# Split-operand scores and head-laid keys for three of four token groups in the first 16-head attention of a fused transformer kernel

## The chip, the cores and the metric

The kernel runs on one core of one Trainium2 chip. The metric is the device time of one execution in microseconds (us); less is better. Before the change it is 921.34 us, the median of three runs (920.03 to 923.55).

A core has engines that run beside each other, each with a queue of its own: TensorE (PE in the profile; its weight loads are PEld), VectorE (DVE), ScalarE (ACT), GpSimd (POOL) and SyncE (SP), which here only issues DMAs. They share an on-chip memory of 128 partitions, and TensorE writes into a second, small one, PSUM, from which VectorE and ScalarE evict.

## The reference

Tokens `x` [32, 64, 128] (32 sequences of 64 tokens) and a context of the same shape go through four blocks, each an attention over the context and a feed-forward part, each added to `x` after a layernorm:

```python
x = x + L0_xattn(layernorm(x), ...);  x = x + L0_ffn(layernorm(x), ...)
x = x + L1_xattn(layernorm(x), ctx);  x = x + L1_ffn(layernorm(x), ...)   # mixture of experts
x = x + L2_xattn(layernorm(x), ctx, ctx);  x = x + L2_ffn(layernorm(x), ...)   # quantized
x = x + L3_xattn(layernorm(x), ctx, ctx);  x = x + L3_ffn(layernorm(x), ...)   # top 2 of 8 experts
```

The change is in `L2_xattn`, the first of two attentions with 16 heads of 8 channels: queries, keys and values are 128-channel projections with bias; in each sequence, each head takes softmax(q·k/√8 + mask) over the 64 keys (the mask is causal in this block), multiplies by the values, and the result is projected by `Wo`. All is float32.

## The kernel before

**Tiling.** The 2048 tokens are 4 groups (g = 0 to 3 in the code, groups 1 to 4 in the text) of 4 tiles of 128 tokens; a tile holds two sequences. `x` stays on chip throughout. `heads_xattn` runs a 16-head block: for each group `heads_inputs` (L1205) makes queries, for each tile `heads_tile` (L1230) does the attention. `i` is 0 for this block and 1 for the second one of the kind, which uses the same code.

**Context.** `heads_context` (L1148) makes, for a group, the values `hv` (a split product at L236 by `mm3`, masked on VectorE at L1173) and by `heads_keys` (L1127) the keys `hk`: one product for each half of the channels (L1134), evicted by ScalarE with the bias (L1144). The keys stand in [channel, token] layout, 64 channels (8 heads) for each of two halves, and twice along the partitions, once for each sequence of a tile. `hv`'s constant columns are set on GpSimd (L1156, L1157).

**Queries.** `queries` (L1196) normalises a group on VectorE (L183), turns it on TensorE (L204) and copies it on ScalarE (L1201, `hqnT`). `heads_inputs` multiplies it by `Wq` (L1222) and evicts four pieces of 64x256 into `hq`: for each half one on VectorE (L1226) and one on ScalarE (L1227), in places such that each sequence's queries meet only that sequence's rows. The rest of `hq` is zero, set once by two memsets (L1124).

**Tile.** GpSimd builds `kb` (L1244): the tile's keys times a mask of heads, 128x1024, so that each of the 8 heads of a half has its own 64 columns with only its 8 channels not zero. Then for each half TensorE adds the mask (L1257, bfloat16) and the score (L1258): queries as the weights, `kb` as the moving operand, 512 columns, in plain float32, which the profile shows as two matmul records. VectorE takes the maximum (L1259) and subtracts it (L1260), ScalarE takes the exponential of both halves (L1261), TensorE transposes 8 blocks (L1268), ScalarE copies them (L1269), TensorE multiplies by the values (L1275), VectorE divides by the sums (L1283, L1284). At a group's end the result is turned (L204), copied (L1298, `hoT`), projected by `Wo` (L1305) and added (L1299, L1306).

**Split products.** Elsewhere the kernel writes a float32 number as a high part, rounded to the type float32r, and a low remainder, and takes three products, `mm3` (L233): high·high, low·high, high·low, each one matmul (the rows L236 and L917).

**Order.** Parts of the work are generators. `interleave` (L98) keeps three tiles in flight here and puts steps of later work (`K.behind`: next group's inputs, weights of the next stage) between them. Over that, the tile framework plans the order on each engine from a modelled timeline; `in_turn` pins the order of a few instructions. The stage before (the mixture of experts, with lines such as L917 to L1016) and this one overlap at their border. Loads go out on SP; the last layer's expert weight `W_raw` is loaded and split (L1490 to L1492) within this stage.

Of the kernel before, what the change touches and what calls it, by code (L numbers as in the profile page):

```python
# [18 lines left out]
F32 = mybir.dt.float32  # L19
# [1100 lines left out]
def heads_room(K, pool):  # L1120

    K.hq = [pool.tile([P, 2, GT, 2, S], F32, name=f"hq{i}") for i in range(2)]
    for t in K.hq:
        K.nc.gpsimd.memset(t, 0.0)  # L1124


def heads_keys(K, pool, i, g, tags):  # L1127

    nc = K.nc
    kT = pool.tile([P, 2, GT, S], F32, name=f"hk{i}{g}")  # L1130
    for half in range(2):
        ps = bank(K, tags[half], [P, GT, 2, S])
        w = K.wkp[i][:, half, :, :].rearrange("p r f -> p (r f)")
        step = nc.tensor.matmul(ps.rearrange("p t b s -> p (t b s)"), w, K.ctxT[g], start=True, stop=True)  # L1134
        if i:
            in_turn(K, [K.l2_last, step])
            K.l2_last = step
        for b in range(2):
            rows = slice(b * S, (b + 1) * S)
            bias = col(K, f"{HEAD_BLOCKS[i]}_bk2", half)[rows, :]  # L1140
            if i and b in KEY_DVE:
                nc.vector.tensor_scalar(kT[rows, half, :, :], ps[rows, :, b, :], bias, None, ALU.add)
            else:
                nc.scalar.activation(kT[rows, half, :, :], ps[rows, :, b, :], AF.Identity, bias=bias)  # L1144
    K.hk[i][g] = kT


def heads_context(K, pool, tp, g, tags):  # L1148
# [4 lines left out]
    hv = K.hv[g] = pool.tile([P, 2 * GT, 2, 8, 2, 9], F32, name=f"hv{g}")  # L1153
# [4 lines left out]
    heads_keys(K, pool, 0, g, tags)  # L1158
# [22 lines left out]
def heads_pools(K, stack, i, side):  # L1181
    b = HEAD_BLOCKS[i]
    return SimpleNamespace(**{
        n: stack.enter_context(K.tc.tile_pool(name=f"{b}_{n}", bufs=bufs, side=at, reuse_waits="tile"))
        for n, bufs, at in (("op", 2, "left"), ("gp", 2, "left"), ("ep", EP[i], side), ("pp", PP[i], side))
    }, kp=K.kp)
# [9 lines left out]
def queries(K, pool, i, g, tags=("hqn", "hqnT")):  # L1196

    qn = normed(K, pool, K.x[g], "hqn", tag=tags[0], stats=None if i else K.l2ln[g], after=K.queried if g and not i else None)
    ps = turned(K, qn, QN[i])
    qnT = pool.tile([P, GT, 2, S], F32, name="hqnT", tag=tags[1])  # L1200
    K.nc.scalar.copy(qnT, ps.rearrange("p (t b s) -> p t b s", b=2, s=S))  # L1201
    return qnT


def heads_inputs(K, C, g):  # L1205
# [10 lines left out]
    yield  # L1216
    ps = bank(K, QN[C.i], [P, 2, GT, S])
# [6 lines left out]
    for half in range(2):  # L1224
        bias = K.hbq[:, C.i, half : half + 1]
        K.queried = nc.vector.tensor_scalar(hq[0:S, half, :, 0, :], ps[0:S, half, :, :], scale, bias[0:S, :], ALU.mult, ALU.add)  # L1226
        nc.scalar.activation(hq[S:P, half, :, 1, :], ps[S:P, half, :, :], AF.Identity, bias=bias[S:P, :], scale=scale)  # L1227


def heads_tile(K, C, g, t):  # L1230
# [8 lines left out]
    if t == AHEAD[C.i] and g + 1 < NG:  # L1239
        K.behind.insert(0, C.inputs[g + 1])  # L1240
    hq, o = K.hq[g % 2], C.o
    kb = C.kp.tile([P, 2, 8, S], F32, name="kb")
    full = [P, 2, 8, S]
    step = nc.gpsimd.tensor_tensor(  # L1244
        kb, K.hk[C.i][g][:, :, t, :].unsqueeze(2).to_broadcast(full),
        K.head.unsqueeze(1).unsqueeze(3).to_broadcast(full), ALU.mult,
    )
    if C.i:
        in_turn(K, [K.l2bo_step, step])
    K.kb_step = step  # L1250
# [3 lines left out]
    for half in range(2):  # L1254
        ps = bank(K, SCORES[C.i][half], [P, 8, S])
        heads = slice(half * 8, half * 8 + 8)
        nc.tensor.matmul(ps, K.identb, K.masks[C.i], start=True, stop=False)  # L1257
        nc.tensor.matmul(ps, hq[:, half, t, :, :].rearrange("p b s -> p (b s)"), kb[:, half, :, :], start=False, stop=True)  # L1258
        nc.vector.tensor_reduce(nm[:, heads], ps, AX.X, ALU.max, negate=True)  # L1259
        nc.vector.tensor_tensor(e[:, heads, :], ps, nm[:, heads].unsqueeze(2).to_broadcast([P, 8, S]), ALU.add)  # L1260
# [36 lines left out]
    oT = C.op.tile([P, GN], F32, name="hoT")[:, : n * P]  # L1297
    nc.scalar.copy(oT, ps)  # L1298
    step = nc.gpsimd.tensor_tensor(xg, xg, K.hbo[C.i].unsqueeze(1).to_broadcast([P, n, P]), ALU.add)  # L1299
    if C.i == 0 and g < NG - 1:  # L1300
# [184 lines left out]
def l3_ffn_weights(K, pool, tmp):  # L1485
    parts = []
    for name, n, src in (("gate", 8, "L3_ffn_gate_w"), ("W3", 1024, "L3_ffn_weight")):
        hi, lo = (pool.tile([P, n], F32R, name=f"{name}_{part}") for part in ("hi", "lo"))
        raw = tmp.tile([P, n], F32, name=f"{name}_raw")
        K.nc.sync.dma_start(raw, K.ins[src])  # L1490
        in_turn(K, [K.normed, K.nc.vector.tensor_copy(hi, raw)])
        K.nc.gpsimd.tensor_tensor(lo, raw, hi.bitcast(F32), ALU.subtract)  # L1492
# [64 lines left out]
def fused_kernel(ctx: ExitStack, tc: tile.TileContext, ins: dict, out: bass.AP):  # L1557
# [17 lines left out]
    K.hk = [[None] * NG, [None] * NG]  # L1575
    K.moe_stack = ExitStack()
# [9 lines left out]
    with ExitStack() as inner:  # L1586
        late, late_k, K.late_v, x_pool = (
            inner.enter_context(tc.tile_pool(name=n, bufs=1, reuse_waits="tile")) for n in ("late", "late_k", "late_v", "l2_x")
        )
        heads_room(K, late)  # L1590
# [5 lines left out]
        K.kp = ctx.enter_context(tc.tile_pool(name="kp", bufs=KB_BUFS, side="right", reuse_waits="tile"))  # L1596
        wp = ctx.enter_context(tc.tile_pool(name="l3f_w", bufs=1, side="right", reuse_waits="tile"))
        with ExitStack() as stack:
            l2_pools = heads_pools(K, stack, 0, "right")
# [4 lines left out]
            K.behind.clear()  # L1604
        l2_stack = ExitStack()
        K.l2p = l2_stack.enter_context(tc.tile_pool(name="l2f_w", bufs=1, side="right", reuse_waits="tile"))
        head_pools = heads_pools(K, inner, 1, "left")
        with tc.tile_pool(name="l2f", bufs=2, reuse_waits="tile") as gp:
            keys = lambda g: heads_keys(K, late_k, 1, g, KEY_TAGS)
# [101 lines left out]
```

## Time and profile before

| | |
|---|---|
| median of 3 runs | 921.34 us (920.03 to 923.55) |
| profiled execution | 922.2 us |
| its span in the profile | 920.5 us |
| mean granted TensorE clock | 0.967 |
| PE / PEld / DVE / ACT / POOL busy | 826.2 / 675.7 / 744.5 / 559.5 / 328.7 us |
| the stage's score products, L1258 | first at 630.2, last at 717.4 us |
| two records of a score product | 0.86 us from the first's start to the next instruction's |
| `kb` on GpSimd, L1244 | x32 (16 in this stage), mean 1.98 us |
| exponential, L1261 | x32, mean 1.06 us |

All are rows of one profiled execution; the span is the time between its first and last instruction, and 1.7 us of the execution lie outside. A row such as "L1258 PE MATMUL s_ps<-kb,hq 128*128 128x512 f32 x2" gives line, engine, operation, output and inputs, shape and count. "<-ACT hq" after a row's idle time names the instruction whose end released it. Matmul records overlap, so what a matmul costs in a full row of them is the distance from start to start.

### The profile page before, as it was taken

The numbers are of one execution on the slowest core, as the hardware profiler recorded it, in microseconds if no ns is written. First come the engines' busy times: TensorE is split into PE (matmuls) and PEld (weight loads), VectorE is DVE, ScalarE is ACT, GpSimd is POOL, SyncE is SP. The second block draws the span as 40 slices with busy tenths as digits, with TensorE's granted clock in tenths as the row PEclk, the third lists the DMA queues.
The fourth block names the chain that finished last, engine by engine and source line by source line (L and its number), as shares of the span: only waits on it lengthen the run. The fifth ranks groups of instructions, "written<-read, shape, count | busy, mean of one in ns | idle before, by whom it ended". The sixth has DMA issues, their size and how long they took to land.

```text
span 920.5 us, 15730 instructions
## 1 busy us (share of the span) xinstructions
PE 826.2 (90%) x5833; PEld 675.7 (73%) x5838; DVE 744.5 (81%) x1888; ACT 559.5 (61%) x1082; POOL 328.7 (36%) x300
## 2 busy tenths in 40 slices
PE   3978999998999998899999799997999789898995
PEld 3878999997998876687787688674676447566673
DVE  5989899698779767877678877789788878779877
ACT  3545676666667579596678767564545483445432
POOL 3744465253323323511040311014465303436342
PEclk9999999999999999999999999998999999899978
DMA  7320000000000000001000000000000000000000
GB/s 188 92 85 21 1 13 13 12 1 1 1 13 1 1 14 0 15 1 33 1 1 1 1 1 1 0 24 1 1 1 1 2 0 1 2 1 1 13 13 23
DMA packets 22669, 13.73 MB, mean 15 GB/s; under 512 B 3008, under 2 KB 21952, under 8 KB 22592
## 3 DMA queue, kind: packets, MB, share of 16 engines
q1 hardware_dynamic: 18320, 10.62, 4.2%
q10 hardware_dynamic: 4272, 2.10, 0.9%
q8 instruction: 46, 0.75, 0.3%
q14 instruction: 31, 0.25, 0.1%
HBM read 11.66 MB, written 1.05 MB: 14 GB/s over the span
## 4 chain that ended last, share of the span: by engine, by line
PE 49%; DVE 27%; ACT 15%; issue 3%; POOL 2%; DMA 2%; SPq 0%; ACTq 0%; DVEq 0%; POOLq 0%
PE c_ps L917 6%; PE g_ps L479 5%; PE s_ps L1258 4%; PE s_ps L445 4%; PE c_ps L236 4%; PE g_ps L236 3%; PE c_ps L1268 2%; PE g_ps L1275 2%; PE t_ps L465 2%; PE s_ps L236 2%; ACT L940 2%; PE t_ps L236 2%; ACT L935 1%; DVE mh_lo L894 1%; DVE nm L447 1%
## 5 line engine op out<-in xcount | busy, mean ns | idle before, releaser
L461 POOL TENSOR_TENSOR e<-e,rs 128x512 f32<-128x512 f32 x64 | 66.0, 1041 | 98.9 <-DVE rs L460 53.4
L161 POOL TENSOR_TENSOR ln_rstd<-ln_rs,neghalf 128x4 f32<-128x4 f32 (+1 forms) x38 | 40.5, 1067 | 144.0 <-DVE ln_rs L169 135.8
L1244 POOL TENSOR_TENSOR kb<-hk,head 128x1024 f32<-128x1024 f32 x32 | 63.2, 1978 | 72.7 <-PE s_ps L1258 57.3
L1258 PE MATMUL s_ps<-kb,hq 128*128 128x512 f32 x128 | 68.9, 623 | 5.4 <-ACT hq L1227 5.2
L445 PE MATMUL s_ps<-kvT,G 128*128 128x128 f32 x512 | 71.6, 277 | 1.8 <-DVE e L451 1.8
L445 PEld LDWEIGHTS s_ps<-kvT,G 128*128 128x128 f32 x512 | 65.6, 192 | 6.0 <-issue 1.8
L917 PE MATMUL c_ps<-mh_hi,w2e_hi 128*128 128x512 f32 x160 | 61.7, 425 | 4.6 <-ACT be L935 2.7
L479 PE MATMUL g_ps<-N,Ct 128*128 128x128 f32 x512 | 61.7, 275 | 0.0
L479 PEld LDWEIGHTS g_ps<-N,Ct 128*128 128x128 f32 x512 | 60.1, 192 | 0.7
L1259 DVE TENSOR_REDUCE nm<-s_ps 128x8 f32<-128x512 f32 x64 | 43.6, 681 | 18.9 <-PE s_ps L1258 18.5
L1269 ACT COPY hpT<-c_ps 128x512 f32<-128x512 f32 x64 | 35.4, 591 | 33.7 <-PE c_ps L1268 33.6
L473 ACT COPY Ct<-c_ps 128x512 f32<-128x512 f32 x64 | 38.2, 598 | 28.6 <-PE c_ps L236 22.7
L469 DVE TENSOR_TENSOR pT_lo<-t_ps,pT_hi 128x512 fp32r<-128x512 f32 x64 | 43.3, 680 | 14.8 <-ACT pT_hi L468 12.5
L1261 ACT ACTIVATE e<-e 128x1024 f32<-128x1024 f32 x32 | 34.0, 1063 | 34.4 <-DVE e L1260 32.0
L1275 PEld LDWEIGHTS g_ps<-hv,hpT 128*64 128x64 f32 x1024 | 36.1, 144 | 22.9 <-issue 8.4
L917 PE MATMUL c_ps<-mh_hi,w2e_lo 128*128 128x512 f32 x160 | 52.1, 403 | 0.0
L894 DVE TENSOR_TENSOR mh_lo<-m,mh_hi 128x1024 fp32r<-128x1024 f32 x32 | 40.4, 1261 | 14.3 <-ACT mh_hi L893 13.4
L452 ACT ACTIVATE e<-e 128x512 f32<-128x512 f32 x56 | 35.4, 640 | 24.5 <-DVE e L451 24.0
L917 PE MATMUL c_ps<-mh_lo,w2e_hi 128*128 128x512 f32 x160 | 49.4, 404 | 0.5 <-DVE mh_lo L894 0.5
L425 ACT COPY G<-g_ps 128x512 f32<-128x512 f32 x60 | 35.9, 598 | 21.4 <-PE g_ps L236 20.4
L468 ACT CAST pT_hi<-t_ps 128x512 fp32r<-128x512 f32 x64 | 37.8, 594 | 17.2 <-PE t_ps L465 10.7
L962 POOL TENSOR_TENSOR be<-be 128x256 f32<-128x256 f32 x16 | 16.9, 1055 | 80.9 <-DVE tg L967 80.3
(519 smaller groups left out, 2689.0 us busy)
## 6 DMA issues: line engine op xcount, KB each, us to landing
kv_tok<-in_x ACTq DMA_DIRECT2D x8, 128.0 KB, 3.3
kv_tok<-in_ctx SPq DMA_DIRECT2D x8, 128.0 KB, 2.9
x<-in_x SPq DMA_DIRECT2D x4, 256.0 KB, 8.2
ctx<-in_ctx SPq DMA_DIRECT2D x4, 256.0 KB, 3.2
w2e_raw<-in_L_ffn_expert_w SPq DMA_DIRECT2D x1, 768.0 KB, 4.4
out<-x SPq DMA_DIRECT2D x3, 256.0 KB, 2.3
WkT<-in_L_xattn_WkT ACTq DMA_DIRECT2D x2, 256.0 KB, 6.4
WqT<-in_L_xattn_WqT SPq DMA_DIRECT2D x2, 256.0 KB, 6.2
```

Source lines behind the costliest of these rows:

```text
L161: K.nc.gpsimd.tensor_tensor(out, v, K.neghalf.to_broadcast(list(v.shape)), ALU.pow)
L236: step = K.nc.tensor.matmul(ps, w[a], x[b], start=start and i == 0, stop=stop and i == 2)
L445: nc.tensor.matmul(ps[:, j, :], G[:, bb, h : h + 2, :].rearrange("p h s -> p (h s)"), kvT[:, bb, :], start=True, stop=True)
L461: nc.gpsimd.tensor_tensor(e, e, rs.unsqueeze(2).to_broadcast([P, 4, P]), ALU.mult)
L469: nc.vector.tensor_tensor(lo, ps, hi.bitcast(F32), ALU.subtract)
L479: nc.tensor.matmul(ps, Ct[:, h, :], C.N[:, h, :], start=(h == 0), stop=(h == 15))
L894: nc.vector.tensor_tensor(lo, m, hi.bitcast(F32), ALU.subtract)
L917: nc.tensor.matmul(ps, K.w2p[part][:, 2 * n + i, cols], x[:, i, :, :], start=first, stop=last)
L1244: step = nc.gpsimd.tensor_tensor(kb, K.hk[C.i][g][:, :, t, :].unsqueeze(2).to_broadcast(full), K.head.unsqueeze(1).unsqueeze(3).to_broadca ...
L1258: nc.tensor.matmul(ps, hq[:, half, t, :, :].rearrange("p b s -> p (b s)"), kb[:, half, :, :], start=False, stop=True)
L1259: nc.vector.tensor_reduce(nm[:, heads], ps, AX.X, ALU.max, negate=True)
L1275: nc.tensor.matmul(po[b * S : (b + 1) * S, j, :, :].rearrange("p r d -> p (r d)"), pT[:, j, b * S : (b + 1) * S], K.hv[g][:, 2 * t + b, C. ...
```

## The change

It touches this block only, and in it the scores of groups 2 to 4; group 1 keeps `kb` and the float32 product.

- **Scores.** For groups 2 to 4 the score is three split products through `mm3` in place of one float32 product.
- **Queries.** In this block all four pieces are evicted on ScalarE. For groups 2 to 4 they go into a plain tile `hqf`; ScalarE copies each to a high part and GpSimd subtracts the low part, into a tile `hqp` with both parts (one for two groups each, zeroed by a memset of 128x2048; groups 2 and 4 share one).
- **Keys.** The keys of groups 2 to 4 are split once for a group (`key_parts`: high copy on ScalarE, low on GpSimd, 128x512 each). Two tiles `kbd` of 128x4096, zeroed once by GpSimd, hold the keys laid out by head for two token tiles each. They are filled by 16 DMAs on SP (8 heads × 2 sequences; 8 partitions × 512 numbers each) for each pair of tiles, in all 6 pairs and 96 DMAs. The twelve `kb` of these groups fall away.
- **Room and order.** Group 1's `kb` shares its place with the last group's values; `hqnT` and `hoT` have one buffer in place of two; the second block's keys take the places of the split keys, and its query tiles are zeroed when its groups begin; the last layer's expert weight is loaded and split in two halves of 512 columns; some `in_turn` pins are dropped, and normalising of group 2 no longer waits for the queries of group 1.

The diff, cut to its core:

```diff
+def key_rooms(K, pool):
+    K.kbd = []
+    for n in range(2):
+        K.kbd.append(zero(K, pool.tile([P, 8, 2, 2, 2, S], F32R, name=f"kbd{n}")))
+        if n == 0:
+            key_parts(K, 1)
+        yield
+
+def key_parts(K, g):
+    kT = K.hk[0][g]
+    parts = K.hks[g] = K.late_k.tile([P, GT, 2, 2, S], F32R, name=f"hks{g}", tag=f"hks{g}")
+    K.nc.scalar.copy(parts[:, :, 0, :, :], kT)
+    K.nc.gpsimd.tensor_tensor(parts[:, :, 1, :, :], kT, parts[:, :, 0, :, :].bitcast(F32), ALU.subtract)
+
+def lay_keys(K, g, pair):
+    kb = K.kbd[pair % 2]
+    for h in range(8):
+        for b in range(2):
+            rows = slice(b * S + 8 * h, b * S + 8 * h + 8)
+            K.nc.sync.dma_start(kb[rows, h, :, :, :, :].bitcast(F32), K.hks[g][rows, 2 * pair : 2 * pair + 2, :, :, :].bitcast(F32))
+    return kb
...
 def heads_inputs(K, C, g):
...
+        if C.i == 0:
+            for b in range(2):
+                rows = slice(b * S, (b + 1) * S)
+                out = hqf[rows, half, :, :] if parts else hq[rows, half, :, b, :]
+                K.queried = nc.scalar.activation(out, ps[rows, half, :, :], AF.Identity, bias=bias[rows, :], scale=scale)
+                if parts:
+                    hi, lo = (hqp[rows, part, half, :, b, :] for part in range(2))
+                    nc.scalar.copy(hi, out)
+                    nc.gpsimd.tensor_tensor(lo, out, hi.bitcast(F32), ALU.subtract)
+            continue
...
 def heads_tile(K, C, g, t):
...
+    parts = C.i == 0 and g > 0
+    if parts:
+        if t % 2 == 0:
+            K.kb = lay_keys(K, g, t // 2)
+        kb = K.kb
+    else:
...
+        if parts:
+            queries = tuple(hq[:, part, half, t, :, :].rearrange("p b s -> p (b s)") for part in range(2))
+            mm3(K, ps, queries, tuple(kb[:, :, t % 2, part, half, :] for part in range(2)), False, True)
+        else:
+            nc.tensor.matmul(ps, hq[:, half, t, :, :].rearrange("p b s -> p (b s)"), kb[:, half, :, :], start=False, stop=True)
...
-    if C.i == 0 and g < NG - 1:
+    if (C.i, g) == (0, 0):
         in_turn(K, [K.kb_step, step])
...
-        raw = tmp.tile([P, n], F32, name=f"{name}_raw")
-        K.nc.sync.dma_start(raw, K.ins[src])
-        in_turn(K, [K.normed, K.nc.vector.tensor_copy(hi, raw)])
-        K.nc.gpsimd.tensor_tensor(lo, raw, hi.bitcast(F32), ALU.subtract)
+        for cols in [slice(at, min(at + 512, n)) for at in range(0, n, 512)]:
+            raw = tmp.tile([P, cols.stop - cols.start], F32, name=f"{name}_raw")
+            K.nc.sync.dma_start(raw, K.ins[src][:, cols])
+            in_turn(K, [K.normed, K.nc.vector.tensor_copy(hi[:, cols], raw)])
+            K.nc.gpsimd.tensor_tensor(lo[:, cols], raw, hi[:, cols].bitcast(F32), ALU.subtract)
```

## The prediction

> **What bounds it now.** I read the busy times first, then the chain of work that ended last, then the stage alone.
>
> ```profile
> PE 826.2 (90%) x5833; PEld 675.7 (73%) x5838; DVE 744.5 (81%) x1888; ACT 559.5 (61%) x1082; POOL 328.7 (36%) x300
> ...
> PE 49%; DVE 27%; ACT 15%; issue 3%; POOL 2%; DMA 2%; SPq 0%; ACTq 0%; DVEq 0%; POOLq 0%
> ```
>
> TensorE is busy nine tenths of the span, but only half of the chain that sets the end is its own; VectorE and ScalarE hold most of the rest. So work taken off TensorE pays only where neither of these is late. The table by stretches shows the stage (first score product at 630, last at 718, in us from the span's start):
>
> ```profile
> 622.00:640.00 18.00, 11.84 (x49) 6.42 (x49) 15.85 (x32) 7.89 (x14) 9.72 (x12) 0.81 0.01 1
> 640.00:660.00 20.00, 19.82 (x183) 13.90 (x182) 17.04 (x39) 11.18 (x18) 9.92 (x7) 1.00 0.00 1
> 660.00:680.00 20.00, 20.00 (x208) 14.45 (x208) 15.63 (x39) 10.71 (x19) 9.16 (x6) 1.00 0.01 2
> 680.00:700.00 20.00, 19.12 (x192) 13.28 (x192) 18.59 (x47) 8.01 (x13) 13.83 (x11) 1.00 0.00 1
> 700.00:722.00 22.00, 21.07 (x222) 14.07 (x221) 17.84 (x45) 11.45 (x18) 7.76 (x6) 1.00 0.01 1
> ```
>
> Columns: length, then busy us of PE, PEld, DVE, ACT, POOL, the granted clock, DMA. From 640 TensorE is full (19.1 to 20.0 of 20), VectorE next (15.6 to 18.6). Only the start is different, and TensorE's waits from 615 to 731 name it:
>
> ```profile
> PE s_ps L1258 <- ACT hq L1227: 5.2, 1, 5.2
> PE s_ps L1257 <- DVE e L1260: 1.3, 3, 0.8
> PE n_ps L1222 <- ACT hqnT L1201: 0.9, 1, 0.9
> ```
>
> One wait of 5.2 us for the first queries; after it waits add up to some 3 us in 100.
>
> **The products.** The timeline shows how matmuls of 512 columns follow each other, in float32 split operands (L917) and in the plain float32 score (L1258):
>
> ```profile
> 614.72 0.62 PE L917 MATMUL c_ps<-mh_hi,w2e_lo 128*128 128x512 f32 x2
> 615.18 0.63 PE L917 MATMUL c_ps<-mh_hi,w2e_hi 128*128 128x512 f32 x2
> 615.65 0.62 PE L917 MATMUL c_ps<-mh_hi,w2e_lo 128*128 128x512 f32 x2
> ...
> 641.20 1.02 PE L1258 MATMUL s_ps<-kb,hq 128*128 128x512 f32 x2
> 642.06 0.60 PE L204 MATMUL n_ps<-ident,W_inT 128*128 128x128 f32 x4
> ```
>
> Start to start, two split products take 0.465 us, one 0.2325, three 0.70; one float32 score (two records) takes 642.06 − 641.20 = 0.86. The gain is 0.16 for a product, and groups 2 to 4 have 3 × 4 tiles × 2 halves = 24: **−3.8 us** of TensorE. The other bound is the records' own lengths: 3 × about 0.41 (L917, mean 403 to 425 ns) = 1.23 against 2 × 0.59 (L1258's shorter records) = 1.18, so +0.05 × 24 = +1.2. Pipelined matmuls overlap, so I take the pacing. The split keys are read in runs of 64 columns; the trace has no split product of that layout.
>
> **The start.** Queries are evicted one half on VectorE (L1226), one on ScalarE (L1227), and ScalarE's stood behind VectorE's: ScalarE was idle 15.3 us over eight L1227 rows, released by L1226. Now all four follow the product on ScalarE, 0.47 each (L1227), idle there from 623.9 to 629.6. The first score can start at about 627 instead of 630.2. But in the built program's order the second score tile now follows the tail of the MoE stage and the next queries, which VectorE still paces (15.85 of 18), and VectorE gets 1.7 us of next-group work earlier (normalising, 4 tiles at 1.06, and the low context part, 0.68). Following the rows through, group 2 begins 0.8 to 1.4 us earlier: **−1.1**. Ends: 0 (VectorE takes all) and −6.1 (5.2 + 0.9, all kept).
>
> **VectorE and GpSimd.** VectorE loses eight evictions of about 0.42. GpSimd loses twelve key blocks of 1.98 (L1244), −23.8; it gains two zeroed key tiles of 4096 columns at four times the 0.94 of a 1024-column memset (7.5), two query tiles of 2048 (3.7), twelve low query parts of at most 0.77 (a subtraction of 128x256; 9.2) and three low key parts of 1.3 (3.9): +24.3. So it is as busy as before, but earlier. Beside a key block VectorE's normalising slows, 2.13 us for four tiles at 696.35 against 1.02 to 1.10 alone; that goes: **−1.1**. Ends: 0, and −3 if each of the three groups gains so.
>
> **ScalarE.** It gains 8 evictions × 0.47, 12 high query parts × 0.47, 3 high key parts × 0.6: 11.2 us on 54.8 of 111. It has room, but the work comes in bursts where a group changes: four evictions, four casts, four key evictions and a key part stand ahead of an exp (L1261, 1.06) which the transposes need. I follow one late exp in group 2: **+1.5** on TensorE. From group 2 on a group's first score waits for an eviction, a cast (0.47) and a subtraction (up to 0.77) in a row, 1.24 more than for an eviction. At the change from group 3 to 4, where an exp and other evictions stand in front, TensorE's waits of before (0.34 at 701.31 and 0.25 at 702.20) become about 2.5 by my count of the rows: **+1.9**. Ends for both together: 0 (score tiles in flight cover them) and +6 (as much at each group).
>
> **The keys' DMAs.** Each pair of tiles needs 16 transfers within the on-chip memory, of 8 rows × 2 KB = 16 KB, all issued from SP; six pairs, 96. No row of before shows such a transfer. SP's small loads stand at 34.44, 34.91 and 35.39, and at 374.76 and 375.22: 0.46 to 0.48 apart; ends 0.37 (414.43 to 414.80) and 0.68 (373.60 to 374.28). Landing of small loads takes 1.6 to 2.5. So a pair takes 16 × 0.48 + 2 = 9.7 us (ends 7.5 and 13.4). In the built program each transfer waits for the landing of the eighth before it, so a landing of over 8 × 0.48 = 3.8 would stretch the row too. What is queued on SP behind these waits: only the next pairs, and the second half of the last layer's expert weight, which is loaded between groups 3 and 4 and waits for GpSimd to have read the first half (684 in before, L1492), so group 4's first pair cannot go before that. A pair can start when the pair before the last has been read, and a tile takes TensorE about 5 us. Following it through: zeroing ends near 637.4, the low key part of group 2 near 644.7, its first pair lands near 654 and is needed near 658; the later ones land 3 to 6 us ahead. I cost them at **0**; the cover is that slack. Behind a score that waits stand, on TensorE, the next tiles' masks, transposes and value products, and through them VectorE. TensorE has to wait on the several semaphores of a pair: about 4 waits × 51 ns (event rows on PE's sequencer) × 6 = 1.2 at most, I take **+0.6**.
>
> A rule speaks against this. The Trainium skill, "DMA: Bandwidth & Descriptors", section "Measured (HBM→SBUF, 128 partitions, SWDGE, issued from GpSimd)", says that transfers under 64 KB are dominated by descriptors and should be batched; its section "Anatomy of one DMA — SWDGE (gpsimd) path" gives a fixed 2.0 us for each. If these added up one after another, a pair would take 16 × 2.04 = 33 us, an estimate from that page, and the sum would end about 100 us later. The loads issued 0.48 apart above overlap their landings, which speaks for 9.7; whether transfers within the on-chip memory do so, no run here shows.
>
> **Sum.** −3.8 − 1.1 − 1.1 + 1.5 + 1.9 + 0.6 = −2.0. From the second feed-forward on (731) the program's order is the same, so the difference is kept. The profiled execution took 922.2 (span 920.5 and 1.7 around it); it becomes 920.2. The median of the three runs is 0.9 below the profiled one: **919.3**.
>
> **Rivals.** About 0.5% (4.6 us) is what a measurement here can tell from no change.
> - *Larger gain* (chance 0.22): the start's 6.1 us stay won, the products' 3.8 too, and the bursts are covered: −5 to −12. For it: the 5.2 us are the stage's only large idle. Against: VectorE at 15.85 of 18 there, which still has the MoE tail to end.
> - *Slower, the DMA issue on SP* (0.18): if an issue with its share of landing takes over 0.70 us, a pair takes over 13 us and eats its slack; from there each 0.1 us costs 16 × 0.1 = 1.6 for a pair, 9.6 for six. At 0.8 to 0.95: +8 to +22, so 929 to 943. For it: the loads at 373.60 (0.68), untried transfers, one queue. Against: the 0.48 of most.
> - *The query chain becomes the wait* (0.13): ScalarE and GpSimd are late at each group, the +6 in place of 3.4, and the start's gain goes: 0 to +5, 921 to 926.
> - *It does not do what it says* (0.07): three split products on strided keys cost what the float32 one costs (+1.2 in place of −3.8): 922 to 925.
> - *Forecast* (0.40): −1 to −5, 916.3 to 920.3.
>
> Faster by over 0.5%: 0.08 of the forecast and 0.22, together 0.30. Slower: 0.18, 0.04 of the query chain, 0.01 of the last, together 0.23. The rest 0.47. The range takes the larger gain down to −11 and the DMA case up to +11, leaving out about 0.16: 910 to 932. The forecast's own range is 916 to 920.5.
>
> **What would show it.** TensorE's start to start over three L1258-kind products: 0.70, or more. The wait for queries of 5.2 gone. SP's issues 0.45 to 0.5 apart, landings 2 us; a TensorE wait released by a DMA before a score of groups 2 to 4 would prove the slower rival, and its length gives its price. An exp waiting behind query casts shows the bursts. GpSimd near 56 us in the stage, VectorE some 5 below. A difference beyond 731 would prove me wrong about the rest. I am wrong in kind if the DMA packets slow other engines, which no row here could tell.

## The result, and the profile after

After the change the kernel takes 927.55 us (median of 6 runs, 926.0 to 929.51), before 921.63 on the same chips (6 runs, 920.03 to 923.55): ratio 1.0063, interval 1.0046 to 1.0080. It is 0.6% slower, by 5.9 us. The forecast was 919.3, so the direction was wrong; the time lies in the range.

The profiled execution took 926.0 (span 924.3), the fastest of the six, so its trace explains 3.8 us, not all 5.9. The stage, from the end of the mixture of experts to the second feed-forward's first transposes, went from 114.6 to 120.4 us (+5.8), what follows from 184.1 to 182.6, what precedes from 621.8 to 621.3. From the page after, busy times and the chain's shares by engine:

```profile
PE 827.5 (90%) x5859; PEld 681.6 (74%) x5862; DVE 747.9 (81%) x1881; ACT 569.1 (62%) x1105; POOL 326.8 (35%) x309
...
PE 51%; DVE 25%; ACT 16%; issue 3%; DMA 2%; POOL 2%; SPq 1%; ACTq 0%; DVEq 0%; POOLq 0%
```

Totals hardly move. The stage's table after, with the stretches and columns of before (length, busy PE, PEld, DVE, ACT, POOL, granted clock, DMA share, GB/s):

```profile
622.00:640.00 18.00, 11.45 (x44) 6.06 (x44) 15.89 (x27) 8.30 (x19) 12.57 (x10) 0.81 0.01 1
640.00:660.00 20.00, 18.78 (x144) 12.63 (x145) 16.69 (x35) 13.00 (x20) 14.33 (x16) 1.00 0.08 16
660.00:680.00 20.00, 19.72 (x220) 15.69 (x218) 16.11 (x42) 11.18 (x21) 5.01 (x6) 1.00 0.13 25
680.00:700.00 20.00, 19.00 (x215) 15.57 (x216) 17.38 (x40) 11.41 (x18) 6.16 (x7) 1.00 0.17 38
700.00:722.00 22.00, 20.76 (x209) 15.75 (x209) 15.14 (x41) 11.82 (x21) 8.05 (x9) 0.84 0.09 17
```

Two rows differ in kind. From 640 to 660 TensorE does 1.04 us less and 144 matmul records instead of 183: the stage starts late. From 700 the granted clock is 0.84 where it was 1.00. TensorE's longest waits after, from 615 to 731 (us in total, times, longest):

```profile
PE n_ps L204 <- DVE x L1017: 2.0, 1, 2.0
PE n_ps L249 <- DVE w_in L137: 1.9, 1, 1.9
PE c_ps L1347 <- ACT e L1340: 1.3, 2, 1.0
PE s_ps L1337 <- ACT hq L1283: 1.2, 1, 1.2
```

The wait of 5.2 for the first queries is 1.2 now (the forecast had it gone), but the first score starts at 629.9 instead of 630.2: others took its place. VectorE's timeline after shows the largest:

```profile
631.99 0.69 DVE L1338 TENSOR_REDUCE nm<-s_ps 128x8 f32<-128x512 f32 x1 [1.17 <-PE s_ps L1337]
632.59 0.41 DVE L984 SCALAR_TENSOR_TENSOR xnext<-step,xnext 128x256 f32<-128x256 f32 x1
633.41 0.69 DVE L1338 TENSOR_REDUCE nm<-s_ps 128x8 f32<-128x512 f32 x1 [0.40 <-PE s_ps L1337]
634.02 4.19 DVE L183 TENSOR_SCALAR hqn<-x,ln_mv,ln_rstd 128x128 f32<-128x128 f32 x4
638.67 1.44 DVE L1002 TENSOR_SCALAR halt<-halt 128x256 f32<-128x256 f32 x1 [0.46 <-ACT halt L1001]
...
642.50 1.28 DVE L1339 TENSOR_TENSOR e<-s_ps,nm 128x512 f32<-128x512 f32 x2
```

The maxima of the two halves of group 1's first tile are ready at 632.7 and 634.1, but their subtractions (L1339) come only at 642.5. Before, maximum and subtraction are neighbours:

```profile
632.65 0.67 DVE L1259 TENSOR_REDUCE nm<-s_ps 128x8 f32<-128x512 f32 x1
633.25 0.40 DVE L984 SCALAR_TENSOR_TENSOR xnext<-step,xnext 128x256 f32<-128x256 f32 x1
633.59 0.67 DVE L1260 TENSOR_TENSOR e<-s_ps,nm 128x512 f32<-128x512 f32 x1
```

Tile 2's score moves from 635.7 to 643.9, group 2's first from 653.3 to 662.7, in these rows of before and after:

```profile
653.33 1.02 PE L1258 MATMUL s_ps<-kb,hq 128*128 128x512 f32 x2
662.68 1.64 PE L236 MATMUL s_ps<-kbd,hqp 128*128 128x512 f32 x6
```

So from the stage's start to group 2's first score it takes 41.4 us where it took 31.5, and from there to the stage's end 79.0 where it took 83.1: the whole loss lies ahead of group 2.

Between the maximum and the subtraction stands the normalising, 4.19 us where four tiles take 1.02 to 1.10 alone, and the end of the mixture of experts (L1002 to L1017). The normalising lies beside this GpSimd row after:

```profile
630.96 7.11 POOL L1128 MEMSET kbd<- 128x4096 f32 x2 [5.39 <-DVE step L983]
```

The longest of the four normalising instructions takes 3.61 us, as long as one memset (3.59); the shortest 0.35. "SBUF — State Buffer" of the Trainium skill, section "SBUF: two separate sides", calls the ports that VectorE and GpSimd share an exclusive lock: where a VectorE instruction needs them, the one that starts first holds them for the whole instruction, with the other blocked. These rows agree. Which of the two holds the subtraction, VectorE's work or something else, they don't tell.

**The clock.** In these stretches of the timeline of after (same columns) the clock is the column before the last two:

```profile
622.70:626.10 3.40, 1.05 (x4) 0.44 (x4) 3.40 (x7) 0.03 (x1) 2.83 (x5) 1.00 0.00 0
626.10:629.50 3.40, 1.98 (x8) 0.79 (x8) 3.40 (x11) 1.24 (x3) 0.00 (x0) 0.51 0.00 0
...
704.60:708.10 3.50, 2.41 (x25) 1.54 (x24) 0.17 (x1) 3.26 (x7) 2.59 (x5) 0.99 0.12 23
708.10:714.90 6.80, 6.80 (x33) 4.66 (x32) 4.63 (x9) 1.64 (x2) 0.60 (x1) 0.50 0.11 22
...
738.80:742.20 3.40, 0.55 (x5) 0.56 (x6) 3.37 (x8) 1.49 (x2) 1.65 (x1) 1.00 0.00 0
742.20:745.60 3.40, 3.18 (x11) 1.65 (x11) 2.39 (x6) 1.45 (x3) 0.00 (x0) 0.50 0.00 0
```

The clock halves in whole steps of 3.41 us, each time after a step that TensorE's records filled only in part (0.16 to 0.68 of it in the three places shown). The stage holds 7.2 us of half clock before (626.8 to 633.6 and a little of 736.0 to 739.4) and 17.1 after: 626.1 and 708.1 for 6.8 each, 731.9 for 3.4. If TensorE does half its work then, the additional 9.9 us cost 5.0 of the 5.8, an estimate. The remaining 0.8 would be what it lost in waits less what it saved in products.

### The profile page after: what moved, and what is told of

It reads as the page before. It is cut to its first block, busy times and chain, and to the rows that moved or that the text cites. A ratio compares the mean times of both kernels' runs of the same rounds, so it can differ in the third digit from the quotient of the medians.

```text
span 924.3 us, 15939 instructions
## 1 busy us (share of the span) xinstructions
PE 827.5 (90%) x5859; PEld 681.6 (74%) x5862; DVE 747.9 (81%) x1881; ACT 569.1 (62%) x1105; POOL 326.8 (35%) x309
## 4 chain that ended last, share of the span: by engine, by line
PE 51%; DVE 25%; ACT 16%; issue 3%; DMA 2%; POOL 2%; SPq 1%; ACTq 0%; DVEq 0%; POOLq 0%
PE c_ps L917 5%; PE g_ps L479 5%; PE s_ps L445 4%; PE c_ps L236 4%; PE g_ps L236 4%; PE s_ps L236 3%; PE s_ps L1337 3%; PE g_ps L1354 3%; PE t_ps L236 2%; PE t_ps L465 2%; PE c_ps L1347 2%; ACT L940 2%; DVE mh_lo L894 2%; DVE m L892 1%; ACT L935 1%
## 5 line engine op out<-in xcount | busy, mean ns | idle before, releaser
L1348 ACT COPY hpT<-c_ps 128x512 f32<-128x512 f32 x64 | 34.8, 591 | 31.4 <-PE c_ps L1347 31.2
L1340 ACT ACTIVATE e<-e 128x1024 f32<-128x1024 f32 x32 | 34.0, 1064 | 30.9 <-DVE e L1339 28.5
L1319 POOL TENSOR_TENSOR kb<-hk,head 128x1024 f32<-128x1024 f32 x20 | 38.1, 1907 | 36.1 <-PE s_ps L1337 33.2
L468 ACT CAST pT_hi<-t_ps 128x512 fp32r<-128x512 f32 x64 | 37.7, 594 | 16.7 <-PE t_ps L465 10.2
L236 PE MATMUL g_ps<-latT_hi,A_hi 128*128 128x256 f32 x120 | 38.9, 324 | 7.6 <-DVE latT_hi L213 4.8
L893 ACT CAST mh_hi<-m 128x1024 fp32r<-128x1024 f32 x32 | 33.4, 1045 | 19.8 <-DVE m L892 18.2
```

Source lines behind the costliest of these rows:

```text
L236: step = K.nc.tensor.matmul(ps, w[a], x[b], start=start and i == 0, stop=stop and i == 2)
L1319: step = nc.gpsimd.tensor_tensor(kb, K.hk[C.i][g][:, t, :, :].unsqueeze(2).to_broadcast(full), K.head.unsqueeze(1).unsqueeze(3).to_broadca ...
```

## The experiments

**Theories.** *Order and rooms* (mine after reading the trace; a tile's room is the address that it gets): the two zeroed key tiles push the exponentials' tile `e` from address 156096 to 131520 (bytes in a partition of the on-chip memory, in the built program), where the end of the mixture of experts still has its tiles. Tile 1's `e` ends at 135616, and `halt`, written at L1002 and read at L1007, starts at 135392. So tile 1's subtraction must wait for L1007. *VectorE held*: GpSimd's zeroing does it. *ScalarE's load*, *DMA issue*: the forecast's rivals. *Half clock* (later): the emptied steps are a cause of their own. *Key supply* (later): 96 transfers in a row are a second bound.

All times are medians with the interval of the ratio to the kernel before, run on the same chip (921.0 to 922.1). "Stage" and "half" are, from the profiled execution, the stage's length and the half-clock time in it. The edits are shortened to their core.

| kernel | us | ratio | stage | half |
|---|---|---|---|---|
| before | 921.63 | | 114.6 | 7.2 |
| after | 927.55 | 1.0046 to 1.0080 | 120.4 | 17.1 |
| e1_zero_pieces | 930.47 | 1.0058 to 1.0105 | 127.2 | 27.3 |
| e2_old_evict | 937.59 | 1.0141 to 1.0183 | 132.5 | 34.1 |
| e3_lay_once | 927.97 | 1.0038 to 1.0076 | 120.3 | 14.9 |
| e4_ahead1 | 931.39 | 1.0078 to 1.0119 | 124.0 | 27.3 |
| e5_pin_norm | 934.24 | 1.0079 to 1.0167 | 125.6 | 23.9 |
| e6_pin_kbd_late | 932.21 | 1.0089 to 1.0148 | 126.0 | 20.5 |
| e7_scalar_evict_only | 922.88 | 0.9994 to 1.0031 | 116.2 | 10.1 |
| e8_f32_laid | 930.67 | 1.0073 to 1.0116 | 124.4 | 14.6 |
| e9_zero_scalar | 932.35 | 1.0112 to 1.0158 | 130.5 | 27.3 |
| e10_zero_dma | 929.16 | 1.0076 to 1.0126 | 123.7 | 17.1 |
| e11_rooms_only | 931.04 | 1.0075 to 1.0126 | 122.3 | 20.1 |
| e12_exp_rooms | 928.25 | 1.0037 to 1.0078 | 123.2 | 20.5 |
| e13_before_pad | 929.22 | 1.0041 to 1.0094 | 124.2 | 15.2 |
| e14_high_only_f32 | 926.87 | 1.0029 to 1.0074 | 120.7 | 10.2 |
| e15_rooms_padded | 932.06 | 1.0068 to 1.0121 | 122.5 | 23.5 |
| e16_before_filled | 920.07 | 0.9971 to 0.9999 | 114.8 | 3.4 |
| e17_after_filled | 928.52 | 1.0053 to 1.0085 | 121.1 | 17.1 |
| e18_key_rooms | 929.48 | 1.0061 to 1.0116 | 122.9 | 30.7 |

**e1: zeroing in pieces** of 512 columns.

```diff
-    K.nc.gpsimd.memset(t, 0.0)
+    for at in range(0, n, 512): K.nc.gpsimd.memset(t[:, at : at + 512], 0.0)
```

> The changed kernel, but the two key tiles and the query tiles are zeroed by memsets of 512 columns (8 and 4 of them) in place of one of 4096 or 2048. Theory A (a VectorE normalising of on-chip data waits for the end of the GpSimd instruction beside it): the four normalisings that took 4.19 us from 634.0 take 2 or less, the first tile's exponential comes 2 to 3 us earlier, the time falls by 1 to 3 us to 924.5 to 926.5. Theory B (the two only share bandwidth, by the number of elements): 4.19 us as before, the time within 1 of 927.5.

No relief, and the time misses both numbers. GpSimd's row in this kernel:

```profile
631.39 7.52 POOL L1128 MEMSET kbd<- 128x512 f32 x16 [4.62 <-DVE step L983]
```

The longest normalising instruction is now 4.77 us, against 0.47 for a piece. If the lock of the page's rule went to VectorE after each instruction, it would have waited at most that 0.47; here the memsets followed each other, and the normalising instruction ended at 639.0, as the row did (638.9).

**e2: the old evictions**, half on VectorE again.

```diff
-    K.queried = nc.scalar.activation(out, ps[rows, half], Identity, bias, scale)
+    K.queried = (that) if b else nc.vector.tensor_scalar(out, ps[rows, half], scale, bias, mult, add)
```

> The changed kernel, but in this block one half of the queries is evicted on VectorE again and one on ScalarE. Theory A (the loss sits in VectorE's waits for GpSimd at the start and in a late query chain with a halved clock at group 4, not in ScalarE's load): between 925 and 929. Theory C (ScalarE's added evictions are the loss): 924 or less.

10 us worse than the change, outside both numbers: ScalarE's load is no cause. In the change's order, evicting on ScalarE helps.

**e3: keys laid out once.** 64 of the 96 transfers are left out, so groups 3 and 4 score against group 2's keys.

```diff
-    K.kb = lay_keys(K, g, t // 2)
+    K.kb = lay_keys(K, g, t // 2) if g == 1 else K.kbd[t // 2]
```

> The changed kernel, but the keys are laid out by DMA for group 2 alone; groups 3 and 4 read group 2's keys, so 64 of 96 transfers are left out and the scores of those groups are computed with the wrong keys. Theory D (the transfers cost the time: SP busy without a pause at 0.67 us an issue, and the packets slow the engines): 922 or less. Theory A (every pair landed before it was needed): within 1.5 of 927.5.

Nothing is gained: in the order that the change has, DMAs cost nothing. After, SP issues them in a row:

```profile
646.08 44.92 SPq L1161 DMA_DIRECT2D kbd<-hks  x64
691.10 0.38 SPq L1570 DMA_DIRECT2D W_raw<-in_L_ffn_weight  x1
691.60 21.44 SPq L1161 DMA_DIRECT2D kbd<-hks  x32
```

They stand 0.67 apart (32 in 21.44), not 0.48, and land 1.7 after their issue. By these figures the pairs land 0.8 to 4.2 us ahead of their first score, and no wait of TensorE ends with one. But six pairs at 16 × 0.67 make 64 us, about as long as groups 2 to 4: this bound is hidden only while the stage is late.

**e4: next group's inputs a tile earlier.**

```diff
-AHEAD = (2, 2)
+AHEAD = (1, 2)
```

> The changed kernel, but in this block the next group's inputs are started one tile earlier (AHEAD 1 in place of 2). Theory A: the first score of group 4 no longer waits for its query parts (1.1 us of TensorE gaps at 705 to 707), the halved clock at 708 to 715 goes, and the time falls by 3 to 5 us, to 922.5 to 924.5. Rival (ScalarE's burst only moves to another place and stalls an exponential there): within 1.5 of 927.5.

The half clock at group 4's start shrinks from 6.8 to 3.4 us (711.3), but 3.4 each come at 643.1 and 690.8, and it is no faster than the change.

**e5, e6: pins.** e5 puts the normalising of group 3's tokens behind a subtraction of the first tiles; e6 also puts the second zeroing behind the low key part.

```diff
-queries(..., after=K.queried if g > 1 and not i else None)
+queries(..., after=K.taken if g > 1 and not i else None)   # e5, e6; taken: the subtraction
+        in_turn(K, [low_key_part, second_zeroing])         # e6
```

> The changed kernel, with one pin of order: VectorE's normalising for groups 3 and 4 is not issued before the last softmax subtraction written ahead of it (the pin of the kernel before, behind VectorE's query eviction, lost its hold when that eviction moved to ScalarE). Theory A (the normalising for group 3 stands on VectorE at 634 to 638 behind GpSimd's memsets, ahead of the first tile's subtraction, and so holds up group 1): the wait of 4.19 us goes, the first exponential comes 3 to 4 us earlier, first score of group 1 to first score of group 2 falls from 32.8 to 29 to 30, time 923.5 to 925.5. Rival (the tail of the stage before and the halved clock set the start whatever stands there): within 1 of 927.5.

> The same pin, and the second key tile is zeroed after the low key part of group 2, in place of right after the first. Theory A: the 1.4 us of VectorE's halting step at 638.7 beside GpSimd go too; 922.5 to 925. Rival: no change against the pin alone, or slower by the 3.5 us memset if it now delays a low part that a transfer waits for.

Neither is faster than the change, and e5's VectorE timeline refutes *VectorE held* as what delays the subtraction:

```profile
633.71 0.69 DVE L1338 TENSOR_REDUCE nm<-s_ps 128x8 f32<-128x512 f32 x1 [0.68 <-PE s_ps L1337]
639.40 0.40 DVE L1002 TENSOR_SCALAR halt<-halt 128x256 f32<-128x256 f32 x1 [5.00 <-ACT halt L1001]
...
642.38 0.42 DVE L1017 TENSOR_TENSOR x<-t_ps,x 128x256 f32<-128x256 f32 x1 [0.65 <-PE t_ps L1016]
642.72 1.28 DVE L1339 TENSOR_TENSOR e<-s_ps,nm 128x512 f32<-128x512 f32 x2
```

The normalising is gone from here, VectorE does nothing for 5 us with both maxima ready, and the subtraction still starts at 642.7, right after L1017. In VectorE's order it stands behind the end of the mixture of experts, whatever else stands there.

**e7: only the evictions**, in the kernel before.

```diff
-    K.queried = nc.vector.tensor_scalar(hq[0:S, half, :, 0, :], ...)
+    K.queried = nc.scalar.activation(hq[0:S, half, :, 0, :], ...) if C.i == 0 else (that)
```

> The kernel before, with only the query eviction of this block moved to ScalarE. Forecast's term (first score 2 to 3 us earlier, of which 1.1 stays): 919.5 to 921. If VectorE's normalising, freed of its pin, goes ahead of the first tile's softmax here too: 922 to 925.

The first score comes at 625.7, 4.5 us earlier, and the time stays (12 runs; the profiled one, 927.04, is the slowest of them). The second tile's score is at 637.2, not before 635.7: the gain ends at the tail of the mixture of experts. A part of this is the pin: it stood behind VectorE's eviction, and without it group 2's normalising (2.69 us at 628.89) goes ahead of that tail, as the second number expects. So taking 4.5 us off the wait was worth nothing here; with the pin kept it was not run.

**e8: laid keys with a float32 product**, no query or key parts.

```diff
-    mm3(K, ps, queries, (kb_high, kb_low), False, True)
+    nc.tensor.matmul(ps, hq[...], kb[:, :, t % 2, half, :], start=False, stop=True)
```

> The changed kernel without the split: keys of groups 2 to 4 laid out by the same 96 transfers (half as long), but as plain float32, one float32 score product in place of three split ones, no high and low parts of queries and keys, key tiles half as wide. If the split chain (casts on ScalarE, subtractions on GpSimd, the wait at group 4) costs more than the 3.5 us of TensorE that it saves: 924 or less. If the split is a gain: 928 to 931.

No faster than the change, but it doesn't price the split: its own smaller tiles put the normalised queries on constants that the stage before still reads (L1005). Inconclusive.

**e9, e10: zeroing elsewhere**, on ScalarE and by a DMA.

```diff
-    K.nc.gpsimd.memset(t, 0.0)
+    K.nc.scalar.copy(t, nil.to_broadcast([P, n]))                # e9
+    K.nc.sync.dma_start(t, nil.unsqueeze(1).to_broadcast([P, n // 256, 256]))   # e10
```

> The changed kernel, but its two key tiles are zeroed by ScalarE (a copy of a zero column, 4096 columns each) in place of GpSimd. Theory A (VectorE is held by GpSimd's zeroing at the start of group 1): the four normalisings that took 4.19 us beside the zeroing fall to about 1.1, the first exponential comes some 3 us earlier, and the time is 923 to 925; ScalarE pays some 2 x 3.7 us there, of which up to 2 us may reach the path. Theory O (the new order and rooms at the start make the loss, whoever zeroes): 927 to 929. Theory K (what is gained at one place is lost again to a half-clock stretch elsewhere): the first exponential earlier, yet 926 to 930.

> The changed kernel, but its two key tiles are zeroed by a DMA each, from a small zero tile (2 MB on the chip for each tile), so that neither GpSimd nor ScalarE does it. Theory A: as with ScalarE but without its price, 922 to 925, the normalisings at 1.1 us. Theory O: 927 to 929. If the transfers themselves are slow (over 15 us for both), the high and low keys' first transfers wait for them, and group 2's first score comes late: over 930.

e9 takes 932.35, more than any of its numbers. With e10 the key tiles' zeroing has left GpSimd and group 1, from its first score to group 2's, takes 27.5 instead of 32.8 us. But tile 2's score stays at 643.8 and the time doesn't fall: the zeroing costs something at the start, but taking it away alone gains nothing.

**e11, e15: rooms only.** e11 has GpSimd's key blocks and float32 products everywhere, no zeroing and no DMA; from the change it keeps the evictions, the rooms, the single buffers and the dropped pins. e15 adds 4 KB to move the query tiles off the constants.

```diff
+    kb = (K.kp if C.i else K.kdp).tile([P, 2, 8, S], F32, name="kb", bufs=2)   # e11, e15
+    x_pool.tile([P, 1024], F32, name="pad_left")                              # e15
```

> The kernel with float32 score products and keys laid out by DMA, but with the keys made by GpSimd's block product again in every group, as before the change: what is left of the change is queries evicted on ScalarE, the new rooms (one shared key tile in group 1, single tiles for turned queries and turned outputs) and the dropped pins. Nothing is zeroed for keys and nothing is laid by DMA. Theory A: the loss goes with the zeroing, 921 to 924. Theory O: the loss stays, 928 to 931, as with the laid keys in float32 (930.7).

> The kernel with keys by block product and float32 scores in the changed rooms (931.0), with an unused tile of 4 KB that shifts the queries' tiles off constants which the end of the MoE stage reads. Theory R (that kernel's slowness was a collision of rooms as well, another one): 920 to 925. If its slowness comes from single buffers, the shared key tile or the dropped pins: 928 to 932.

The loss stays without zeroing, transfers and split products. But neither run prices the change's own rooms: in both, `e` is at 156096 again, as in the kernel before, and in e11 the normalised queries lie on the same constants as in e8. e15 removes that collision, and its 932.06 misses the number of *Theory R* and is that of its rival (single buffers, shared key tile, dropped pins): TensorE waits 5.75 us until 639.7 for the mixture of experts (L984), with the clock at half from 624.5 to 645.0. So these parts of the change can cost as much as the rooms. Which of them does, no run separates.

**e12: the key tiles below the exponentials'**, no instruction changed.

```diff
+    if (i, n) == (0, "ep"):
+        K.kdp = [... tile_pool(name=f"kdp{j}", bufs=1, side="right") for j in range(2)]
-    K.kdp = ... tile_pool(name="kdp", bufs=1, side="right")
```

> The changed kernel, with one thing moved: the two key tiles get their rooms after (below) those of the exponentials, so that the exponentials no longer lie on tiles that the end of the MoE stage reads. No instruction is added or taken away. Theory R (rooms): VectorE's first subtraction goes back to about 634 (642.5 in the changed kernel), the first exponential to about 637 (645.3), group 2's first score to about 654 (662.7), and the time is 917 to 923. The rival O (the order comes from the evictions on ScalarE, the dropped pins or the zeroing): no change, 926 to 929. The second key tile now lies on the MoE stage's last tiles and is zeroed later; if group 2's second pair then comes late, a TensorE wait of some us before its score eats a part: 921 to 925.

The order at the start returns (second tile at 636.9, later ones at 639.6, 642.5 …), as the theory said, but not the time. Group 2's first score is even later, 664.2: its split keys, which lie on weights of the mixture of experts, are made from 645.0 on (640.2 in the change), its first transfer is issued at 650.0, and issues run until 717.8. The key supply has become the bound at group 2's start; in e14, with the same rooms, TensorE waits 0.54 us for a transfer at 674.8.

**e13: the kernel before with an empty tile** of 24 KB that pushes `e` to the address that it has after.

```diff
+    tc.tile_pool(name="pad_right", bufs=1, side="right").tile([P, 6144], F32, name="pad_right")
```

> The kernel before, with an empty tile of 24 KB in front of the exponentials' room, which nothing writes or reads: it only shifts the exponential tiles to the addresses that they have in the changed kernel. Theory R: the first subtraction moves behind the end of the MoE stage (to about 641), the second score tile too, and the time is 927 to 932. Rival O: an unused tile costs nothing, 920 to 923.

An unused tile costs 7.4 us (929.22 against 921.85), no less than the whole change; `e` is at 131520, as in the changed kernel. In its VectorE timeline the maximum and the subtraction part as they do after:

```profile
631.57 0.69 DVE L1259 TENSOR_REDUCE nm<-s_ps 128x8 f32<-128x512 f32 x1 [0.36 <-PE s_ps L1258]
...
637.04 0.47 DVE L1007 SCALAR_TENSOR_TENSOR xoT<-t_ps,bf,halt 128x256 f32<-128x256 f32 x1
...
639.40 0.42 DVE L1017 TENSOR_TENSOR x<-t_ps,x 128x256 f32<-128x256 f32 x1
639.74 1.28 DVE L1260 TENSOR_TENSOR e<-s_ps,nm 128x512 f32<-128x512 f32 x2
```

L1007 and L1017 belong to the stage before. The subtraction writes where L1007 reads `halt`, so it must follow L1007; the rows up to L1017 stand between them in VectorE's planned order. That is the mechanism shown by itself.

**e14: e12 with one float32 product** of the high parts; the products with low parts are left out.

```diff
-    mm3(K, ps, queries, ...)
+    nc.tensor.matmul(ps, hq_high.bitcast(F32), kb_high.bitcast(F32), start=False, stop=True)
```

> The kernel with exchanged rooms, in which each score of groups 2 to 4 is one float32 product of the high parts in place of three split ones; the low parts are still made and laid out, but left out of the product. It is the price of the products alone, everything else equal: if TensorE's 24 x 0.15 us reach the end, 3 to 4 us slower than with exchanged rooms; if TensorE has slack, within 1 us.

926.87 against e12's 928.25: not slower, though each product takes TensorE longer. In these rooms, where the transfers bind, what split products save doesn't reach the end.

**e16, e17: filler.** Mask products without use ahead of the first score and of the second feed-forward's transposes, 20 and 15 in before, 6 and 15 in after.

```diff
+    for _ in range(n):
+        step = K.nc.tensor.matmul(ps, K.identb, K.masks[0], start=True, stop=True)
+        in_turn(K, [after, step]); after = step
```

> The kernel before, with useless products of the mask (each overwritten at once by the real one, or never read): 20 ahead of the first score, where TensorE waits 5.2 us for the queries, and 15 ahead of the first transposes of the second feed-forward network, where it waits 4.0 us. Theory K (a window of 3.41 us that is too little busy makes the next one run at half the clock, and costs up to 1.7 us): the half-clock stretches at 626.8 (6.8 us) and 736.0 (3.4 us) shrink or go, and the time falls by 1.5 to 4 us, to 917.5 to 920. Rival (the half clock falls into waits and costs nothing, or the fillers delay): no change or up to 1 us slower, 921 to 923.

> The changed kernel, with 6 such useless products ahead of the first score (its wait there is 1.2 us, after a half-empty window that stays) and 15 ahead of the first transposes of the second feed-forward network (wait 3.6 us). Theory K: the second half-clock window at the start (629.5) and the one at 742.2 go, the ones at 708.1 and 731.9 stay: 2 to 3.5 us faster than the changed kernel, 924 to 925.5. Rival: 927 to 928.5.

In e16 the steps stay filled and the clock full:

```profile
622.70:626.10 3.40, 3.40 (x20) 1.57 (x21) 3.40 (x4) 0.00 (x0) 3.40 (x4) 1.00 0.00 0
626.10:629.50 3.40, 3.03 (x14) 1.18 (x11) 3.40 (x9) 0.47 (x1) 1.90 (x7) 1.00 0.00 0
```

The kernel before gains 1.95 us by doing more (12 runs, 920.07 against 922.02), at the edge of what can be told; it is the fastest version. The profiled execution (922.04) doesn't show where: its stage takes 114.8 us with 3.4 of half clock, before 114.6 with 7.2. In e17 the half clock only moved (626.3, 643.4, 687.8, 735.5), and the time is the rival's.

**e18: e12 with group 2's split keys in a room free early.**

```diff
-    parts = K.hks[g] = K.late_k.tile(...)
+    parts = K.hks[g] = (K.late_k1 if g == 1 else K.late_k).tile(...)
```

> The kernel with exchanged rooms, and one more tile moved: the split keys of group 2 get a room that is free early, so that they are ready before the first key tile is zeroed. No instruction is added or taken away. Theory R+S (rooms decide the start, and the keys' supply is the second bound behind it): SP's first issue comes at about 636 to 638 instead of 650, group 2's first score at 653 to 657 instead of 664.2, and the time falls by 5 to 9 us to 919 to 923, level with the kernel before or under it; the gain of the split products (3.5) then shows only as far as SP's 64 us of issues leave room. Rival (neither decides; the half-clock windows and VectorE eat it again wherever it falls): 926 to 929.

Group 2's first score is at 653.1, as expected: 31.2 us after the stage's start, as in the kernel before (31.5), where the change takes 41.4. Only tiles have moved, so the rooms made that delay. But the key supply still binds: the second key tile, now on the last tiles of the mixture of experts, is zeroed late,

```profile
648.98 3.52 POOL L1128 MEMSET kbd<- 128x4096 f32 x1
```

so the second pair's transfers run from 652.5 to 663.0, and its first score, at 665.2, comes about 0.5 us after the last landing. TensorE is full until 679. Then:

```profile
677.40:680.90 3.50, 1.95 (x41) 1.64 (x40) 2.86 (x8) 2.32 (x6) 1.85 (x3) 1.00 0.13 26
680.90:684.30 3.40, 2.75 (x18) 2.13 (x18) 1.80 (x7) 3.25 (x8) 3.24 (x5) 0.50 0.12 24
684.30:687.70 3.40, 3.40 (x32) 2.40 (x30) 0.32 (x1) 1.17 (x3) 3.10 (x5) 0.50 0.28 79
```

One wait of 1.92 us at 681.3 for group 3's evicted queries (L1285), then 10.2 us of half clock; as much stands at 626.3 and at 728.7. With half of its half-clock time taken off, an estimate, the stage is 107.6, against before's 111.0: 3.4 shorter, about the products' 3.6. With it, 122.9. The time missed its number and lies just above the rival's.

## Why the prediction was wrong, step by step

- **The start (−1.1) is the step that failed.** It said that VectorE gets "1.7 us of next-group work earlier" and group 2 begins 0.8 to 1.4 us earlier. Group 2's first score came 9.4 us later, and the 4.1 us that the rest of the stage gained don't pay for it. The step saw that the second score tile follows the tail of the mixture of experts and still counted a gain. What it left out is where the new tiles lie: it took the order of the built program as given but did not ask what moved it. e13 prices such a shift at 7.4 us in the kernel before, e12 shows the order return, and e18 the start. That the rooms alone make the 5.9 us isn't shown: with them mended, e12 and e18 gain nothing at the end. The end at −6.1 counted the wait for the first queries at its full length: e7 took 4.5 us of it away and gained nothing. And the 15.3 us that ScalarE was idle are of both 16-head blocks; in this one it was 8.1 us over four rows.
- **GpSimd's work "as busy as before, but earlier"** was costed at nothing. Earlier was the cost: 7.1 us of memsets beside the first tile's normalising, 4.2 us for 1.1. The VectorE gain (−1.1) was thus lost at the start, though late key blocks did go (GpSimd 640 to 722: 40.7 to 33.6). By e5 and e10 it isn't what decides the time.
- **The products (−3.8): the size was right.** Three with the mask stand 0.92 apart where one float32 product with its mask stood 1.07: 0.15 × 24 = 3.6. TensorE's busy time over the stage, with time at half clock counted half, falls by less, from 98.7 to 96.7. But it isn't the path in the rooms of e12: e14.
- **The burst (+1.5) and the query chain (+1.9)** show as 0.97 at 680.9 (for an exponential, L1340) and as 0.25, 0.31 and 0.54 at 705 to 707: the waits are smaller than forecast, 2.1 for 3.4. Behind the second came half clock for 6.8 us, by the estimate above some 3.4 more.
- **DMA waits (+0.6) and DMAs (0)**: no TensorE wait ends with a transfer. The spacing was 0.67 for the 0.48 that I took, just under the 0.70 from which the slower rival decides, and the pairs' slack was 0.8 to 4.2 us for the 3 to 6 forecast. That rival didn't happen, but e12 shows it one step away.
- **"The difference is kept" from 731 on**: 1.5 us shorter, with 28.5 us of half clock there instead of 33.9; the program's order is the same.
- **Half clock** was no term at all, though the trace of before shows it (0.81 in the first row). Over the 20 profiled executions the stage's length goes as 113.8 + 0.47 × its half-clock time (correlation 0.84). That is a relation, not a proof: late work empties steps too. e16 (−1.95 us) points to a price, but its profiled execution doesn't show it.

The outcome lies in no rival's range: above the *query chain* (to 926) and below the *DMA issue* (from 929). None of the rivals named the mechanism.

**What stays open.** No version with split products beat the kernel before. Undoing a cost uncovered another each time: zeroing (e10), rooms (e12), the first pair's keys (e18), and then the second pair's, the start of group 3 and the clock. Whether e18 with these mended would win was not tried, nor were the dropped pins and single buffers, which e15 makes suspect, put back one by one. Nor does a trace here show where the slower executions of after lose their further 2 us.

## What to carry to other kernels

Before costing a change's instructions, look where its new tiles push the old ones: a write to an address that an earlier stage still reads is a wait that no instruction of the diff shows, and an unused tile is the experiment that prices it. Where other engines pace a stage, less TensorE work makes its gaps wider, not the stage shorter; look at the filling of each 3.4-us step, not at the total. When one cost is undone, read the trace for the next bound before counting the gain.

## What the runs showed of the hardware

- **Half clock follows an unfilled step, not only a long pause.** Steps are 3.413 us long and run through. Over the 20 profiled executions, after a step at full clock whose TensorE records fill less than 0.40 of it, the next was at half clock in 117 of 117 cases; 0.40 to 0.50: 74 of 81; 0.50 to 0.55: 33 of 74; 0.55 to 0.75: 48 of 397; above: 22 of some 4200. Full clock returned only after a step filled to 0.83 or more. "TensorE: Matmul & The Clock Gate" of the Trainium skill, section "Why this matters for your kernels", asks for no idle gap over about 3 us; here 0.25 + 0.31 + 0.54 us within one step were followed by 6.8 us of half clock.
- **A row of short memsets on GpSimd holds a VectorE instruction as a long one does**: 4.77 us beside pieces of 0.47 (e1), 3.61 beside one of 3.59.
- **Transfers of 16 KB within the on-chip memory** are issued 0.67 us apart on SP and land 1.7 after the start of their issue; issue and landing overlap.
